# An image's six convolution pieces over four rounds: one, two, two, one

## The chip, the cores and the metric

The kernel runs on one core of a Trainium2 chip. The metric is the time on the device in microseconds, the median of three runs. All arithmetic is in 32-bit floats. Five engines work side by side, each with its own queue of instructions: TensorE (PE, with weight loads as PEld) for matrix products, VectorE (DVE), ScalarE (ACT) and GpSimd (POOL) for work on elements, and SyncE (SP), which here issues most of the DMA transfers. They wait for each other by semaphores.

## What is computed

The input is 16 images of 192 channels and 56 x 56 points. First comes a Swin block (windows of 7 x 7, shifted by 3, six heads), then a convolution whose weights depend on the image. Cut to what matters here:

```python
# layer 0: Swin block
h = roll(layernorm(x), (-3, -3))            # over channels
q, k, v = windows(h) @ qkv_w + qkv_b        # 64 windows of 49 tokens an image
a = softmax(q @ k.T * scale + bias + mask) @ v
x1 = x + roll(a @ proj_w + proj_b, (3, 3))
x2 = x1 + gelu(layernorm(x1) @ fc1_w + fc1_b) @ fc2_w + fc2_b

# layer 1: depthwise 3 x 3 convolution, weights made from the image
t = relu(batchnorm(mean(x2, over=(H, W)) @ w1.T))
wt = (t @ w2.T + b2).reshape(192, 3, 3) * MASK   # only 4 of 9 taps are not masked:
                                                 # three above, one to the left
out = depthwise_conv(x2, wt) + bias
```

The convolution of an image needs the mean over the whole image, and so it can start only when the Swin block of that image is finished.

## The kernel before

An image is handled in four steps of 14 rows (two rows of windows), 64 steps in all. The main loop is a software pipeline over rounds `i` from 2 to 65. In round `i` the MLP of step `i-2`, the attention of step `i`, the query, key and value products of step `i+1` and the norms of other steps are interleaved. The loop sets the order of the instructions on each engine by hand.

```python
for i in range(2, NS + 2):                     # NS = 64
    A, B_, C, D = pairs                        # four pairs of PSUM banks, in turn
    cs = conv_ready(2)                         # <- the line of the change
    ys = [conv_begin(*c) for c in cs[:1]]      # first piece: start, on ACT
    if has(i + 1):
        norm1_scale(i + 1, dvs.pop(0), nc.vector)   # win <- x,dv on DVE

    def after():
        ys.extend(conv_begin(*c) for c in cs[1:])   # second piece: start, on ACT
        for c, y in zip(cs, ys):
            conv_rest(*c, y)                        # three taps each, on DVE

    if (i + 3) % STEPS == 0 and (i + 3) // STEPS < B:    # STEPS = 4
        b = (i + 3) // STEPS
        images[b] = load_x(b, nc.sync)         # three images are held at a time

    def between():
        singles[0] = banks(f"st_{i}", C)
        keys.update(stats_of(i))               # PE: st <- x,sel and st <- sq,sel
        if keys:
            var.append(norm_vars(keys))        # ACT: square into dev; DVE: dev <- st,dev
    ...
    mlp_first(i - 2, yns.pop(i - 2), hid, (A, B_, C, D, A, B_), after, between)
    ...
    if has(i):
        top, share = attention_scores(i, *qs.pop(i), (C, D, A, B_))   # PE: sc <- kbd,q
    ...   # products q, k, e; softmax; second half of the MLP (pf); projection (pp); pv
    if (i - 2) % STEPS == STEPS - 1:           # an image's last step: its weights
        pt = taps(b, ...)                      # four matmuls on PE
        convs.append({"b": b, "n": 0})
    ...
    if has(i):
        residual(i, pp, pair1, at)             # DVE
    if has(i + 1):
        v_whole()
        attention_v_out(pvs)                   # vbd <- pv on DVE and ACT
    if has(i):
        norm_squares(f"2_{i}", i, 1, nc.scalar)
    if pt is not None:
        taps_rows(b)                           # DVE copies of border rows
        convs[-1]["wt"] = taps_out(b, convs[-1]["tt"])   # DVE: tw, wt
c = convs.pop()                                # the last image, after the loop
for n in range(6):
    conv_rest(c["b"], c["wt"], n, conv_begin(c["b"], c["wt"], n))
```

The first matrix product of the MLP frames both `after` and `between`:

```python
def mlp_first(i, yn, hid, ks, after, between):
    ...
    for f in range(3):
        take(f)
        long(dsts[f], wf1, cols(f), y0, True)      # PE: ph <- yn,wf
    for f in range(3):
        short(dsts[f], wf1, cols(f), y1, False)
        gelu(f)                                    # ACT: hid <- ph
    after()                                        # the convolution's pieces
    for f in range(3, NFC):
        take(f)                                    # banks that a Gelu has to free
        short(dsts[f], wf1, cols(f), y1, True)
    between()                                      # st, dev
    for f in range(3, NFC):
        long(dsts[f], wf1, cols(f), y0, False)
        gelu(f)
```

An image's convolution is cut into six pieces of 14 rows: four on the tall tile `x0` (channels 0 to 127, all 56 rows) and two on the half-height tile `x1` (the other 64 channels, its two halves side by side on 128 partitions). A piece takes one instruction on ACT (the first tap with the bias) and three on DVE; pieces three and five (counted from zero) have a small copy besides. The result goes out by DMA.

```python
def conv_ready(k):
    ready = []
    while k and convs and "wt" in convs[0]:
        c = convs[0]
        ready.append((c["b"], c["wt"], c["n"]))
        c["n"] += 1
        k -= 1
        if c["n"] == 6:
            convs.pop(0)
    return ready

def conv_begin(b, wt, n):
    kc, lo = (0, n * PR) if n < 4 else (1, (n - 4) * PR)     # PR = 14
    y = work.tile([128, PR, IMG], F32, tag="y", name=f"y_{b}_{n}", bufs=3)
    nc.scalar.activation(y, images[b][kc][:, lo : lo + PR], AF.Identity,
                         bias=cb[kc], scale=wt[:, kc, 1:2])
    return y

def conv_rest(b, wt, n, y):
    ...
    def tap(t, dst, src):
        nc.vector.scalar_tensor_tensor(
            dst, src, wt[:, kc, t : t + 1], dst, ALU.mult, ALU.add)
    tap(0, y[:, :, 1:], up[:, :, : IMG - 1])
    tap(2, y[:, :, : IMG - 1], up[:, :, 1:])
    ...
    tap(3, y[:, :, 1:], cur[:, :, : IMG - 1])
    ...                                                       # DMA to out
```

The weights of image `b` are made at the end of round 4b+5. Its pieces run in rounds 4b+6, 4b+7 and 4b+8, two in each; round 4b+9 has none. In that round the load of image b+3 is issued, into the buffers that image `b` held.

Of the kernel before, what the change touches and what calls it, by code (L numbers as in the profile page):

```python
# [36 lines left out]
def tile_swin_then_dynamic_conv(  # L37
# [45 lines left out]
    def banks(name, k):  # L83
        return psum.tile([128, 2, 512], F32, tag=f"pair{k}", name=name)
# [14 lines left out]
    def load_x(b, queue):  # L99
        t0, t1 = new_x(b)  # L100
        queue.dma_start(t0[:, 1 : 1 + LAST], x[b, 0:C0, SHIFT:IMG])
        queue.dma_start(t0[:, 1 + LAST : 1 + IMG], x[b, 0:C0, 0:SHIFT])
        queue.dma_start(t1[0:64, 1 : 1 + HALF], x[b, C0:DIM, SHIFT : SHIFT + HALF])
        queue.dma_start(t1[64:128, 1 : 1 + LAST - HALF], x[b, C0:DIM, SHIFT + HALF : IMG])
        queue.dma_start(t1[64:128, 1 + LAST - HALF : 1 + HALF], x[b, C0:DIM, 0:SHIFT])
        return t0, t1
# [206 lines left out]
    def norm1_scale(i, dv, engine):  # L313

        v0, v1 = rows_of(i)
        b4 = dv.rearrange("p h (r c) -> p h r c", c=IMG)
        w0 = win0[:, :, :, 0:N].rearrange("p h w (r c) -> p h r w c", c=WS)
        w1_ = win1[:, :, 0:N].rearrange("p w (r c) -> p r w c", c=WS)
        cut = WS - SHIFT
        for ws, cs, at, n in (  # L320
            (slice(0, NWIN - 1), slice(0, WS), SHIFT, NWIN - 1),
            (slice(NWIN - 1, NWIN), slice(0, cut), IMG - cut, 1),
            (slice(NWIN - 1, NWIN), slice(cut, WS), 0, 1),
        ):
            m = n * (cs.stop - cs.start)

            def wide(v):
                return v[..., at : at + m]

            for h in range(2):  # L330
                engine.tensor_tensor(
                    w0[:, h, :, ws, cs],
                    wide(v0[:, h]).rearrange("p r (w c) -> p r w c", w=n),
                    wide(b4[:, h]).rearrange("p r (w c) -> p r w c", w=n),
                    ALU.mult,
                )
            for h in range(2):
                p = slice(h * 64, h * 64 + 64)
                engine.tensor_tensor(  # L339
                    w1_[p, :, ws, cs],  # L340
                    wide(v1[p]).rearrange("p r (w c) -> p r w c", w=n),
                    wide(b4[p, h]).rearrange("p r (w c) -> p r w c", w=n),
                    ALU.mult,
                )
# [344 lines left out]
    def conv_begin(b, wt, n):  # L689

        kc, lo = (0, n * PR) if n < 4 else (1, (n - 4) * PR)
        y = work.tile([128, PR, IMG], F32, tag="y", name=f"y_{b}_{n}", bufs=3)
        nc.scalar.activation(  # L693
            y,
            images[b][kc][:, lo : lo + PR],
            AF.Identity,
            bias=cb[kc],
            scale=wt[:, kc, 1:2],
        )
        return y  # L700

    def conv_rest(b, wt, n, y):
        kc, lo = (0, n * PR) if n < 4 else (1, (n - 4) * PR)
        xk, cbk = images[b][kc], cb[kc]
        up, cur = xk[:, lo : lo + PR], xk[:, lo + 1 : lo + 1 + PR]

        def tap(t, dst, src):
            nc.vector.scalar_tensor_tensor(  # L708
                dst, src, wt[:, kc, t : t + 1], dst, ALU.mult, ALU.add
            )  # L710

        tap(0, y[:, :, 1:], up[:, :, : IMG - 1])
        tap(2, y[:, :, : IMG - 1], up[:, :, 1:])

        if n in (3, 5):
            p = slice(0, 128) if kc == 0 else slice(64, 128)
            nc.vector.tensor_copy(
                y[p, LAST - 3 * PR, :], cbk[p].broadcast_to([p.stop - p.start, IMG])
            )
        tap(3, y[:, :, 1:], cur[:, :, : IMG - 1])  # L720
        halves = [(slice(0, 128), slice(0, C0), lo)]
        if kc:
            halves = [(slice(h * 64, h * 64 + 64), slice(C0, DIM), lo + h * HALF) for h in range(2)]
        for p, c, at in halves:
            k = min(PR, LAST - at)
            nc.sync.dma_start(out[b, c, at + SHIFT : at + SHIFT + k], y[p, 0:k])
            if k < PR:
                nc.sync.dma_start(out[b, c, 0 : PR - k], y[p, k:PR])
# [8 lines left out]
    yns, convs, qs, dvs = {}, [], {}, {}  # L737

    def has(i):
        return 0 <= i < NS  # L740
# [12 lines that stand above are left out]
# [234 lines left out]
    for i in range(2, NS + 2):  # L987
        A, B_, C, D = pairs
        keys = {}


        cs = conv_ready(2)
        ys = [conv_begin(*c) for c in cs[:1]]
        if has(i + 1):
            norm1_scale(i + 1, dvs.pop(0), nc.vector)

        def after():
            ys.extend(conv_begin(*c) for c in cs[1:])
            for c, y in zip(cs, ys):
                conv_rest(*c, y)  # L1000

        if (i + 3) % STEPS == 0 and (i + 3) // STEPS < B:
            b = (i + 3) // STEPS
            images[b] = load_x(b, nc.sync)

        def between():
            singles[0] = banks(f"st_{i}", C)
            keys.update(stats_of(i))
            if keys:
                var.append(norm_vars(keys))  # L1010

        var = []
        hid = one.tile([128, NFC, 2, T], F32, tag="hid", name=f"hid_{i - 2}")
        mlp_first(i - 2, yns.pop(i - 2), hid, (A, B_, C, D, A, B_), after, between)
        for part, dev in var:
            table(AF.Sqrt)
            norm_root(part)


        outs = [lambda: None] * 4  # L1020
        if has(i):
            table(AF.Exp)
            top, share = attention_scores(i, *qs.pop(i), (C, D, A, B_))
        if has(i + 1):
            qs[i + 1], outs = attention_qk(i + 1, C, D, A)
        if has(i):
            top(0)
        outs[0]()
        if has(i):
            top(1)  # L1030
            share(0)
        outs[1]()
        if has(i):
            top(2)
            share(1)
        outs[2]()
        if has(i):
            top(3)
            share(2)
        outs[3]()  # L1040
        if has(i):
            share(3)
        for part, dev in var:
            nc.vector.reciprocal(part, part)
            dvs.update(norm_spread(keys, dev))

        prts = []

        def turn(f):
            for wp in ((), (), (), (0,), (1,), (2, 3))[f]:
                if has(i):
                    prts.append(attention_turn(i, wp, (C, A)[wp % 2]))

        pf = mlp_wide(i - 2, hid, B_, turn)
        mlp_out(i - 2, 0, pf[:, :, :T])
        table(AF.Gelu)
        if 1 in keys:
            yns[i - 1] = norm2_scale(i - 1, dvs.pop(1))  # L1060
        if has(i + 3):
            norm_squares(f"1_{i + 3}", i + 3, 0, nc.gpsimd)
        if has(i):
            o = attention_rows(i, attention_values(i, prts, D, C))
        pf1 = mlp_narrow(i - 2, hid, A)
        mlp_out(i - 2, 1, pf1[:, :T])
        if has(i):
            pp, pair1, p_narrow, p_rest, p_whole = project(i, o, B_, C)
            p_narrow()
            p_rest()  # L1070
        if has(i + 1):
            pvs, v_rest, v_whole = attention_v(i + 1, (D, A))
            v_rest()
        if has(i):
            p_whole()
        b, pt, at = (i - 2) // STEPS, None, lambda: None
        if (i - 2) % STEPS == STEPS - 1:
            pt = taps(b, taps_pool(b), pair1[:, 1] if has(i) else banks(f"t_{b}", C)[:, 0])
            convs.append({"b": b, "n": 0})

            def at():
                convs[-1]["tt"] = taps_hidden(b, pt)

        if has(i):
            residual(i, pp, pair1, at)
        else:
            at()
        if has(i + 1):
            v_whole()
            attention_v_out(pvs)  # L1090
# [3 lines that stand above are left out]
            taps_rows(b)  # L1094
            convs[-1]["wt"] = taps_out(b, convs[-1]["tt"])
        pairs = [C, B_, D, A]
# [77 lines left out]
```

## Time and profile before

| | |
|---|---|
| time, median of 3 runs | 3253.55 us (3251.41 to 3253.6) |
| span of the profiled run | 3251.8 us |
| clock granted to PE, mean | 0.986 |
| a tap of the convolution on DVE (L708) | 288 of them, 314.0 us busy, 1104 ns mean |
| DVE `dev<-st,dev`, 64x392 (L285) | two a round, 0.57 us each |
| HBM traffic | 41.25 MB read, 38.54 MB written, 25 GB/s over the span |

In the profile a group of instructions is named by its line, its engine, and what it writes and reads with buffer numbers left out: `ph<-yn,wf` is the first product of the MLP, `st<-x,sel` the sums for the norms, `dev` the variance, `sc<-kbd,q` the attention's scores, `y<-x,wt,y` a tap of the convolution. Most matmuls have the same line, L92, since a helper issues them, so they are told apart by tile. In a timeline, neighbouring instructions of one kind are put together: the first column is the start in us from the beginning of the span, the second the time to the end of the last of them, and xN their number. In square brackets stands how long the engine was idle before it, and who ended that wait.

### The profile page before, as it was taken

The numbers are of one execution on the slowest core, as the hardware profiler recorded it, in microseconds if no ns is written. First come the engines' busy times: TensorE is split into PE (matmuls) and PEld (weight loads), VectorE is DVE, ScalarE is ACT, GpSimd is POOL, SyncE is SP. The second block draws the span as 40 slices with busy tenths as digits, with TensorE's granted clock in tenths as the row PEclk, the third lists the DMA queues.
The fourth block names the chain that finished last, engine by engine and source line by source line (L and its number), as shares of the span: only waits on it lengthen the run. The fifth ranks groups of instructions, "written<-read, shape, count | busy, mean of one in ns | idle before, by whom it ended". The sixth has DMA issues, their size and how long they took to land.

```text
span 3251.8 us, 64181 instructions
## 1 busy us (share of the span) xinstructions
PE 3123.3 (96%) x26130; PEld 1937.1 (60%) x26130; DVE 2115.2 (65%) x3895; ACT 1887.8 (58%) x2988; POOL 991.6 (30%) x897
## 2 busy tenths in 40 slices
PE   5699999999999999999999999999999999999996
PEld 3556666666656656666666656666665665666653
DVE  5355675766766575685676666576676667667564
ACT  2455665655655665565565565565565666566552
POOL 5333233233223323323323323323323322322220
PEclk9699999999999999999999999999999999999998
DMA  3001011111111202112111201112111121211001
GB/s 99 16 15 51 25 37 51 37 55 31 40 52 32 60 31 61 31 31 56 36 52 40 58 26 40 51 35 56 31 37 55 31 59 32 61 30 32 22 30 45
DMA packets 79123, 135.35 MB, mean 42 GB/s; under 512 B 21766, under 2 KB 61692, under 8 KB 76908
## 3 DMA queue, kind: packets, MB, share of 16 engines
q1 hardware_dynamic: 77266, 128.54, 14.0%
q8 instruction: 206, 3.38, 0.4%
q0 software_dynamic: 1056, 1.92, 0.3%
q10 hardware_dynamic: 506, 0.79, 0.1%
q14 instruction: 89, 0.73, 0.1%
HBM read 41.25 MB, written 38.54 MB: 25 GB/s over the span
## 4 chain that ended last, share of the span: by engine, by line
PE 85%; DVE 9%; issue 2%; POOL 1%; ACT 0%; DMA 0%; SPq 0%; DVEq 0%; POOLq 0%; ACTq 0%
PE pf L92 23%; PE ph L92 19%; PE pp L92 7%; PE pv L92 6%; PE po L92 6%; PE pt L508 4%; PE pq L92 4%; PE sc L92 4%; PE pk L92 4%; PE pe L92 4%; PE st L92 3%; DVE y L708 3%; DVE win L339 1%; DVE vbd L451 1%; DVE x L584 1%
## 5 line engine op out<-in xcount | busy, mean ns | idle before, releaser
L92 PE MATMUL ph<-yn,wf 128*128 128x392 f32 (+1 forms) x3072 | 808.8, 501 | 9.3 <-ACT hid L598 3.5
L92 PE MATMUL pf<-hid,wf 128*128 128x392 f32 (+1 forms) x3072 | 802.8, 494 | 3.5 <-ACT hid L598 2.0
L495 POOL TENSOR_TENSOR prob<-e,tot 113x588 f32<-113x588 f32 x256 | 298.6, 1177 | 1205.6 <-DVE tot L494 1190.0
L92 PEld LDWEIGHTS ph<-yn,wf 128*128 128x128 f32 (+1 forms) x3072 | 424.7, 188 | 365.0 <-issue 83.9
L451 ACT COPY vbd<-pv 49x192 f32<-49x192 f32 x512 | 160.6, 314 | 704.2 <-DVE vbd L451 699.5
L92 PEld LDWEIGHTS pf<-hid,wf 128*128 128x128 f32 (+1 forms) x3072 | 386.3, 164 | 303.7 <-issue 120.0
L644 DVE SCALAR_TENSOR_TENSOR x<-pf,cols,x 128x784 f32<-128x784 f32 (+1 forms) x128 | 106.1, 829 | 537.8 <-PE pf L92 508.7
L598 ACT ACTIVATE hid<-ph,f1b 128x784 f32<-128x784 f32 x384 | 337.2, 913 | 115.1 <-PE ph L92 114.0
L253 POOL TENSOR_TENSOR sq<-sq,sq 64x392 f32<-64x392 f32 x256 | 263.7, 1030 | 369.5 <-ACT sq L247 354.9
L708 DVE SCALAR_TENSOR_TENSOR y<-x,wt,y 128x770 f32<-128x770 f32 x288 | 314.0, 1104 | 16.6 <-ACT y L693 8.4
L350 POOL TENSOR_TENSOR yn<-x,dv 128x784 f32<-128x784 f32 x64 | 119.0, 1859 | 571.3 <-DMA dv<-dev 549.1
L92 PEld LDWEIGHTS pv<-wqkv,win 64*128 64x128 f32 (+1 forms) x2048 | 258.1, 190 | 35.1 <-ACT kbd L405 2.8
L92 PE MATMUL pv<-wqkv,win 64*128 64x192 f32 (+1 forms) x2048 | 274.8, 327 | 3.3 <-ACT kbd L405 2.5
L486 DVE TENSOR_TENSOR e<-e,top 113x588 f32<-113x588 f32 x256 | 267.1, 1043 | 8.9
L92 PE MATMUL pp<-o,wp 128*128 128x392 f32 (+2 forms) x896 | 251.5, 514 | 2.7 <-ACT o L544 2.7
L489 ACT ACTIVATE e<-e 113x588 f32<-113x588 f32 x256 | 176.7, 691 | 132.9 <-DVE e L486 132.9
L238 ACT ACT_TABLE_LOAD x192 | 246.3, 1283 | 3.4
L514 ACT COPY prt<-pt 128x678 f32<-128x678 f32 x256 | 179.3, 727 | 117.2 <-PE pt L508 115.7
L479 DVE TENSOR_TENSOR e<-sc,bias_t 113x588 f32<-113x588 f32 x256 | 179.9, 763 | 100.5 <-PE sc L92 100.3
L508 PEld LDWEIGHTS pt<-ident,prob 113*128 113x128 f32 x1536 | 167.3, 142 | 77.8 <-issue 48.7
L92 PE MATMUL po<-prt,vbd 128*64 128x49 f32 x6144 | 199.9, 225 | 0.0
L92 PEld LDWEIGHTS po<-prt,vbd 128*64 128x64 f32 x6144 | 191.9, 140 | 9.4 <-ACT prt L514 0.6
(146 smaller groups left out, 3987.0 us busy)
## 6 DMA issues: line engine op xcount, KB each, us to landing
dv<-dev SPq DMA_DIRECT2D x1020, 49.0 KB
x<-in_x_dram SPq DMA_DIRECT2D x15, 1484.0 KB
out_dram<-y SPq DMA_DIRECT2D x48, 392.0 KB
out_dram<-y SPq DMA_DIRECT2D x48, 196.0 KB
x<-in_x_dram SPq DMA_DIRECT2D x16, 392.0 KB
x<-in_x_dram SPq DMA_DIRECT2D x15, 350.0 KB
out_dram<-y SPq DMA_DIRECT2D x16, 308.0 KB
out_dram<-y SPq DMA_DIRECT2D x16, 154.0 KB
```

The costliest lines, as they stand in the source:

```text
L92: nc.tensor.matmul(dst, lhs, rhs, start=start, stop=stop, skip_group_check=True)
L238: nc.scalar.activation(junk, eps_t[0:1], func)
L253: nc.gpsimd.tensor_tensor(s0[p, h], s0[p, h], s1[p], ALU.add)
L451: copy(dst, src[s * 64 : s * 64 + N, h, :, :, j, :])
L479: nc.vector.tensor_tensor(e, sc[:PW, :, : HEADS * N], rel, ALU.add)
L486: nc.vector.tensor_tensor(ehs[wp], ehs[wp], t.broadcast_to([PW, 2 * HEADS, N]), ALU.subtract)
L489: nc.scalar.activation(es[wp], es[wp], AF.Exp)
L495: nc.gpsimd.tensor_tensor(prob[wp][:PW, :, 0:N], ehs[wp], t.broadcast_to([PW, 2 * HEADS, N]), ALU.mult)
L508: nc.tensor.transpose(pt[:, a, g * PW : (g + 1) * PW], prob[wp][:PW, h : h + 2, :].rearrange("p h k -> p (h k)"), ident[:PW, :PW],)
L514: nc.scalar.copy(prt, pt[:, :, : 3 * PW])
L598: nc.scalar.activation(hid[:, f], phs[f][:, :, :T], AF.Gelu, bias=f1b[:, f : f + 1])
L708: nc.vector.scalar_tensor_tensor(dst, src, wt[:, kc, t : t + 1], dst, ALU.mult, ALU.add)
```

## The change

In the round in which an image's first piece is due, one piece is taken in place of two. The other rounds still take up to two, so that the six pieces fall on four rounds as one, two, two and one, and the last of them lies in round 4b+9, which had none. It is meant to take work off VectorE in the round that follows the making of the weights. Nothing is added or left out; every instruction stays as it was, and some move to a later round.

```diff
-        cs = conv_ready(2)
+        cs = conv_ready(1 if convs and not convs[0]["n"] else 2)
```

The pieces after the loop, of the last image, are not touched.

## The prediction

> **What bounds the kernel now.** I read the page first, then the list of waits, then the trace cut into rounds, and last the timelines of two rounds side by side.
>
> ```profile
> PE 3123.3 (96%) x26130; PEld 1937.1 (60%) x26130; DVE 2115.2 (65%) x3895; ACT 1887.8 (58%) x2988; POOL 991.6 (30%) x897
> PE 85%; DVE 9%; issue 2%; POOL 1%; ACT 0%; DMA 0%; SPq 0%; DVEq 0%; POOLq 0%; ACTq 0%
> ```
>
> TensorE (PE) is busy for 96% and carries 85% of the chain that ended last. VectorE (DVE) is busy for 65% only and yet holds 9% of the chain: there are places where it decides. The waits view names one that bears on this change:
>
> ```profile
> PE sc L92 <- DVE dev L285: 23.1, 15, 1.5
> ```
>
> The scores' matmuls waited 23.1 us in total for the DVE instruction `dev`, 15 times, 1.5 us each. Fifteen is the number of images whose convolution runs inside the loop (0 to 14), so it happens once an image. To see where, I cut the trace at each start of a group of score matmuls. A stretch then runs from the attention of one round to the first matrix product (`ph`, `st`, `ph`) of the next, in which the pieces run. Columns: stretch, its length, and busy time and count of PE, PEld, DVE, ACT and POOL, then clock, DMA share and GB/s.
>
> ```profile
> 1592.67:1640.34 47.67, 47.67 (x407) 29.66 (x406) 34.04 (x60) 29.78 (x47) 14.85 (x13) 1.00 0.12 32
> 1640.34:1688.02 47.68, 47.68 (x408) 29.69 (x407) 27.00 (x53) 27.92 (x45) 14.84 (x13) 1.00 0.26 75
> 1688.02:1738.40 50.38, 48.61 (x411) 29.93 (x411) 35.89 (x67) 31.27 (x49) 15.07 (x13) 1.00 0.10 29
> 1738.40:1786.08 47.68, 47.68 (x407) 29.67 (x407) 34.05 (x60) 28.28 (x46) 14.85 (x13) 1.00 0.12 36
> ```
>
> These stretches hold the pieces of rounds 32 (two pieces, the image's last), 33 (none), 34 (the next image's first two) and 35 (two more). Two pieces or none, a stretch takes 47.68 us and PE is full: pieces are free there. Only the stretch with an image's first two takes longer, by 2.70 us. There are fourteen more like it: thirteen are within 0.02 us of it, and the last takes 49.72 us against 47.01 us for the stretch after it, 2.71 more. Now PE in the long stretch, and below it DVE and ACT there (start, duration, what, idle before):
>
> ```profile
> 1728.86 1.74 PE L92 MATMUL ph<-yn,wf 64*128 64x392 f32 x8 [0.23 <-ACT hid L598]
> 1730.53 1.52 PE L92 MATMUL st<-x,sel 128*32 128x392 f32 x16
> 1731.87 0.84 PE L92 MATMUL st<-sq,sel 128*32 128x392 f32 x8
> 1732.64 4.22 PE L92 MATMUL ph<-yn,wf 128*128 128x392 f32 x12
> 1738.40 2.24 PE L92 MATMUL sc<-kbd,q 64*64 64x98 f32 x96 [1.54 <-DVE dev L285]
> ```
> ```profile
> 1724.91 0.56 DVE L674 SCALAR_TENSOR_TENSOR tw<-tt,w2n 128x384 f32<-128x384 f32 x1
> 1725.51 0.55 DVE L683 TENSOR_REDUCE wt<-tw 128x8 f32<-128x384 f32 x1
> ...
> 1730.90 6.18 DVE L708 SCALAR_TENSOR_TENSOR y<-x,wt,y 128x770 f32<-128x770 f32 x6
> 1737.11 1.14 DVE L285 TENSOR_TENSOR dev<-st,dev 64x392 f32<-64x392 f32 x2
> ```
> ```profile
> 1732.87 0.99 ACT L283 ACTIVATE dev<-st 64x392 f32<-64x392 f32 x2 [1.51 <-PE st L92]
> ```
>
> `dev` has its inputs when ACT's square is done, at 1732.87 + 0.99 = 1733.86. It starts at 1737.11, because six taps (two pieces of three) stand before it in DVE's queue, and they begin late, at 1730.90, behind the new image's weights (`tw`, `wt`), which only this round computes. In round 32 the same queue is ahead of PE:
>
> ```profile
> 1631.61 5.93 DVE L708 SCALAR_TENSOR_TENSOR y<-x,wt,y 128x770 f32<-128x770 f32 x5
> 1637.58 0.19 DVE L717 COPY y<-cols 64x56 f32<-64x56 f32 x1
> 1637.80 1.02 DVE L708 SCALAR_TENSOR_TENSOR y<-x,wt,y 128x770 f32<-128x770 f32 x1
> 1638.85 1.14 DVE L285 TENSOR_TENSOR dev<-st,dev 64x392 f32<-64x392 f32 x2
> ```
>
> It ends at 1639.99, and the scores start at 1640.34 with no wait.
>
> [...] round 32's last `ph` group is given an end of 1640.42, and the next matmul starts at 1640.34. So I reckon with starts. [...] round 32's first tap starts at 1631.61 while POOL adds squares (1630.52 to 1632.62) and takes 1.84 us; the others take 1.02.
>
> **The change part by part.** Piece counts per image go from 2, 2, 2, 0 to 1, 2, 2, 1. Instructions are the same in number and shape; what moves is one piece out of each first round, one each between the others, and the last into a round that had none.
>
> 1. First round (34 and its like). DVE loses three taps of 1.02 us with gaps of about 0.03: 6.18 / 6 x 3 = 3.09 us. The last tap then ends at 1734.0. ACT's square ends at 1733.86, so `dev` runs from about 1734.05 to 1735.2. What would the scores then wait for? In an undisturbed stretch they follow the last `ph` group's start by 1640.34 - 1636.20 = 4.14 us. Here that group starts at 1732.64, so they may start at 1736.79 instead of 1738.40. `dev` is ready 1.5 us before. The gain is 1738.40 - 1736.79 = 1.61 us: half of the 3.09 us of taps was already beside PE's work.
>
> 2. The rest of the 2.70 us stays, 1.09 us. The taps' weights need four matmuls on PE, 0.4 us. The matmuls of `ph` wait for ACT's Gelu to free banks; ACT does the first piece's start (1.02 us) before the Gelu and comes late from its copies, since DVE is late: `st` starts 8.85 us after the first `ph` (1721.69, shown in the PE timeline as 1730.53) instead of 8.20 us, so 0.65 us. The first piece stays in this round and ahead of the Gelu, so this stays. New length of the stretch: 50.38 - 1.61 = 48.77 us.
>
> 3. Second and third rounds hold two pieces as before: 47.68 us each.
>
> 4. Last round (33, 37 and so on): one piece more on a DVE with 27.0 us busy of 47.7. Round 32 shows that two pieces in this place cost nothing, so one doesn't. ACT's start of a piece (about 1.03 us) also comes before the Gelu, as in round 32, where it costs nothing. Cost 0.
>
> 5. The third image after takes over this image's buffer, and its load is issued in that last round. The order of instructions shows a new wait: the load of the half-height tile `x1` now waits for DVE and ACT, for piece five still reads it; the load of the tall tile has no such wait. Before, the five loads are issued from 1667.78 to 1671.50. After, `x1` can go when the taps of round 33 are done, about 1679.3 + 3 x 1.05 + 0.8 (the first beside POOL) + 0.2 = 1683.5. Its first reader is POOL's square at 1717.86, 34 us later. About 0.8 MB at the 265 GB/s that the trace shows while an image comes in is 3 us. The queue behind it holds nothing urgent: the next copies of `dv` are issued at 1704.89. Cost 0.
>
> 6. The end. Image 14's last piece goes into round 65, in which ACT waits 17.9 us and DVE 25.0 us; image 15's six pieces after the loop are untouched. The taps there may meet POOL's scaling of `yn` (1.83 and 2.09 us from 3193.88), on which PE waits: up to 1 us, once. I count 0.
>
> Sum: 15 first rounds x 1.61 = 24.2 us. 3253.55 - 24.2 = 3229.4 us, 0.7% less.
>
> **The rivals.** First, the whole 2.70 us goes, 40 us in all and 3213 us. That would need the second piece to be what makes the Gelu late; against it, that piece's start on ACT comes after the three Gelus (1730.30 against 1727.90). Second, a first round still bound by DVE: if taps took 1.84 us each, as the one beside POOL, `dev` would end 2.5 us later and nearly all gain would go: 3250 us. Against it, POOL's last addition there ends at 1729.34, before the taps start. Third, the load becomes the wait: a late `x1` holds POOL's squares, then `st`. It has some 30 us in hand; if it did cost 1 us an image, the time would be 3245. Fourth, the piece in the round without pieces costs what it frees: 15 x 1.6 back, no change; rounds 32 and 35 speak against it.
>
> **Range and chances.** All steps are read from stretches that repeat to 0.02 us, and three runs lie within 2.2 us, so the doubt is in steps 2, 4 and 5. A loss of 0.4 us an image gives 6 us more, 3235; a gain of 0.3 us in step 2 gives 4.5 us less, 3225. I take 3225 to 3236. Two per cent are 65 us; PE's work alone forbids that gain. Faster by over 2%: 0.01; within: 0.98; slower: 0.01.
>
> **What would show it.** Right: `sc <- dev` gone from the waits; stretches of 48.8, 47.7, 47.7 and 47.7 us; three taps before `dev` in the first; `x1` loads some 12 us later than the tall tile's with POOL's squares where they were. Wrong: a first stretch of 47.7 (step 2), or of over 49 (step 1), a fourth over 48 (step 4), or a wait of POOL for `in_x_dram` (step 5).

## The result, and the profile after

The changed kernel takes 3229.15 us (median of 4 runs, 3228.76 to 3229.39), the kernel before in the same comparison 3253.57 us. The ratio is 0.9925, 95% interval 0.9908 to 0.9943: 24.4 us or 0.75% less. The prediction was 3229.4 us.

The page of the changed kernel, busy time by engine and the chain that ended last:

```profile
PE 3121.5 (97%) x26130; PEld 1936.5 (60%) x26130; DVE 2130.7 (66%) x3895; ACT 1886.0 (58%) x2988; POOL 992.1 (31%) x897
PE 89%; DVE 3%; ACT 2%; issue 1%; POOL 1%; DMA 0%; SPq 0%; ACTq 0%; DVEq 0%; POOLq 0%
```

The counts of instructions are the same. DVE's share of the chain fell from 9% to 3% while its busy time rose, by 15.5 us: a first hint that it was never DVE's total that mattered. The list of waits no longer has the row in which `sc` waits for `dev`, which stood there with 23.1 us. The stretches of rounds 32 to 35, in the columns used before:

```profile
1581.62:1629.30 47.68, 47.68 (x407) 29.66 (x406) 34.05 (x60) 29.75 (x47) 14.81 (x13) 1.00 0.11 30
1629.30:1676.98 47.68, 47.68 (x408) 29.67 (x407) 31.07 (x57) 28.82 (x46) 14.87 (x13) 1.00 0.26 74
1676.98:1725.75 48.77, 48.54 (x412) 29.91 (x411) 32.92 (x64) 28.82 (x46) 15.05 (x13) 1.00 0.13 35
1725.75:1773.42 47.67, 47.67 (x407) 29.66 (x406) 33.85 (x59) 29.75 (x47) 14.82 (x13) 1.00 0.11 33
```

The second line is the round that had no piece; DVE works 4.1 us more in it, and it is as long as before. The third is the first round of an image: 48.77 us instead of 50.38. PE, DVE and ACT in that stretch:

```profile
1717.82 1.73 PE L92 MATMUL ph<-yn,wf 64*128 64x392 f32 x8 [0.23 <-ACT hid L598]
1719.49 1.52 PE L92 MATMUL st<-x,sel 128*32 128x392 f32 x16
...
1721.60 4.22 PE L92 MATMUL ph<-yn,wf 128*128 128x392 f32 x12
1725.75 2.24 PE L92 MATMUL sc<-kbd,q 64*64 64x98 f32 x96
```
```profile
1719.87 3.13 DVE L708 SCALAR_TENSOR_TENSOR y<-x,wt,y 128x770 f32<-128x770 f32 x3
1723.03 1.14 DVE L285 TENSOR_TENSOR dev<-st,dev 64x392 f32<-64x392 f32 x2
```

Three taps stand before `dev` instead of six. It ends at 1724.17, and the scores follow the last `ph` group after 4.15 us, as in any other round, with no wait in brackets. The 0.23 us before the upper `ph`, from the late Gelu, are still there.

The sum over the loop: 14 first stretches of 1.61 us less and the last with 1.62 us less make 24.16 us. The rest of the 24.5 us between the two profiled spans is 0.40 us at the start, 0.51 us in the last stretch, and 0.45 us the other way: one stretch took 0.57 us more than its like, where before another took 0.12 more. Start and last stretch differ by a few microseconds between profiled runs (the start from 186.7 to 191.8 us, the last stretch from 110.1 to 115.1), so a hit to within 0.3 us in the total is partly luck. The stretches themselves are not. The last stretch goes with how often the granted clock fell to 0.5 for 3.41 us in it, before the last matmul: 110.1 to 111.0 us where it never did, 112.4 to 113.2 where it did once, as before and after the change, and 115.0 or 115.1 where it was low for longer.

### The profile page after: what moved, and what is told of

Same layout as the page of the kernel before. It is cut to its first block, busy times and chain, and to the rows that moved or that the text cites. A ratio compares the mean times of both kernels' runs of the same rounds, so it can differ in the third digit from the quotient of the medians.

```text
span 3227.3 us, 64171 instructions
## 1 busy us (share of the span) xinstructions
PE 3121.5 (97%) x26130; PEld 1936.5 (60%) x26130; DVE 2130.7 (66%) x3895; ACT 1886.0 (58%) x2988; POOL 992.1 (31%) x897
## 4 chain that ended last, share of the span: by engine, by line
PE 89%; DVE 3%; ACT 2%; issue 1%; POOL 1%; DMA 0%; SPq 0%; ACTq 0%; DVEq 0%; POOLq 0%
PE pf L92 23%; PE ph L92 21%; PE pp L92 7%; PE pv L92 6%; PE po L92 6%; PE pt L508 4%; PE pq L92 4%; PE sc L92 4%; PE st L92 4%; PE pe L92 4%; PE pk L92 4%; DVE vbd L451 1%; DVE x L584 1%; ACT hid L598 0%; ACT y L693 0%
## 5 line engine op out<-in xcount | busy, mean ns | idle before, releaser
L708 DVE SCALAR_TENSOR_TENSOR y<-x,wt,y 128x770 f32<-128x770 f32 x288 | 328.7, 1151 | 16.8 <-ACT y L693 8.2
L578 DVE SCALAR_TENSOR_TENSOR x<-pp,cols,x 128x371 f32<-128x371 f32 (+1 forms) x128 | 48.0, 417 | 227.8 <-PE pp L92 227.8
```

The source lines that it names most:

```text
L708: nc.vector.scalar_tensor_tensor(dst, src, wt[:, kc, t : t + 1], dst, ALU.mult, ALU.add)
```

## The experiments

All were timed beside the kernel before. "First stretch" is the one that ends in an image's first round, 50.38 us before and 48.77 us after; the second to fourth follow it.

| pieces, and what else is changed | time, us | first to fourth stretch, us |
|---|---|---|
| 2, 2, 2, 0 (before) | 3253.57 | 50.38, 47.68, 47.68, 47.67 |
| 1, 2, 2, 1 (the change) | 3229.15 | 48.77, 47.68, 47.68, 47.68 |
| 2, 2, 1, 1 | 3253.03 | 50.39, 47.68, 47.68, 47.68 |
| 2, 2, 2, 0, `dev` between the first two pieces | 3230.12 | 48.77, 47.74, 47.68, 47.68 |
| 1, 2, 2, 1, first start behind the Gelus | 3219.18 | 48.12, 47.68, 47.68, 47.68 |
| 0, 2, 2, 2 | 3219.06 | 48.12, 47.68, 47.68, 47.68 |
| 2, 2, 2, 0, first starts behind the Gelus | 3270.81 | 50.39, 49.29 (nine of fifteen), 47.68, 47.68 |
| 1, 3, 2, 0 | 3276.44 | 48.77, 50.52, 47.68 (four: 49.1 to 49.3), 47.68 |
| 1, 3, 2, 0, three taps done again | 3344.53 | 48.77, 53.68, 49.94, 47.68 |
| 1, 2, 2, 1, start behind the Gelus, weights twice | 3222.24 | 48.57, 47.68, 47.68, 47.67 |
| 1, 2, 2, 1, tall tile last | 3226.99 | 48.77, 47.68, 47.68, 47.68 |

The stretches are medians over the images.

**Only the first round had no room.** Two, two, one, one:

```diff
-        cs = conv_ready(2)
+        cs = conv_ready({2: 2, 3: 2, 0: 1, 1: 1}[i % STEPS])
```

> Two, two, one, one: six pieces over four rounds, as many rounds with one piece as in the change, but the first round keeps two. Theory (only the first round had no room): first stretch 50.4 us, the others 47.7 us, time 3253.5 us as before. Rival (it is the spreading over four rounds that pays, wherever the single pieces lie): about 3229 us.

3253.03 us, ratio 0.9997 (0.9988 to 1.0005). The first two stretches:

```profile
1685.68:1736.07 50.39, 48.61 (x411) 29.94 (x411) 35.89 (x67) 31.25 (x49) 15.04 (x13) 1.00 0.13 38
1736.07:1783.75 47.68, 47.68 (x406) 29.67 (x406) 34.03 (x60) 28.25 (x46) 14.83 (x13) 1.00 0.12 36
```

Nothing is gained by a piece in the fourth round as such. What pays is the piece missing from the first. The rival, spreading for its own sake, falls.

**The order in DVE's queue, or its load?** Two, two, two, none, but in the first round the second piece's taps stand after `dev`:

```diff
+        ahead = 1 if cs and cs[0][2] == 0 else 2
 ...
-            for c, y in zip(cs, ys):
+            for c, y in list(zip(cs, ys))[:ahead]:
                 conv_rest(*c, y)
 ...
                 var.append(norm_vars(keys))
+            for c, y in list(zip(cs, ys))[ahead:]:
+                conv_rest(*c, y)
```

> Two, two, two, none as before, but in an image's first round the three taps of the second piece stand after `dev` in DVE's queue. DVE does as much in that round as in the kernel before. Theory (what cost 1.61 us was `dev` standing behind the taps): `dev` starts near 1734.05 on the clock of the trace before and the scores are no longer held by it; the second piece's taps then end some 0.6 us later than DVE would have begun on the scores, which costs up to 0.3 us at the products that reuse those banks: first stretch 48.8 to 49.1 us, time 3229 to 3235 us. Rival (DVE had too much work in that round, in whatever order): the wait only moves to the scores' banks, the stretch and what follows it keep 2.7 us too many, 3253 us.

3230.12 us, ratio 0.9925 (0.9910 to 0.9940): the same gain as the change, though no piece left its round. DVE in the first stretch:

```profile
1719.59 3.13 DVE L708 SCALAR_TENSOR_TENSOR y<-x,wt,y 128x770 f32<-128x770 f32 x3
1722.75 1.14 DVE L285 TENSOR_TENSOR dev<-st,dev 64x392 f32<-64x392 f32 x2
1723.82 3.12 DVE L708 SCALAR_TENSOR_TENSOR y<-x,wt,y 128x770 f32<-128x770 f32 x3
1726.85 2.79 DVE L479 TENSOR_TENSOR e<-sc,bias_t 113x588 f32<-113x588 f32 x4
```

The same six taps, `dev` between them. The first stretch is 48.77 us. DVE begins on the scores 1.39 us after PE's start on them (1725.46), in the changed kernel 0.87 us, and this image's second stretch is 47.75 us instead of 47.68: the whole price of the late taps is 0.07 us. So the cost was `dev` in DVE's queue behind work that nobody waited for, and not too much work for DVE in that round.

**What is left in the first stretch: ACT.** The change, with the start of the first round's piece behind the three Gelus:

```diff
+        early = 0 if cs and cs[0][2] == 0 else 1
-        ys = [conv_begin(*c) for c in cs[:1]]
+        ys = [conv_begin(*c) for c in cs[:early]]
 ...
-            ys.extend(conv_begin(*c) for c in cs[1:])
+            ys.extend(conv_begin(*c) for c in cs[early:])
```

> One, two, two, one, and in an image's first round the start of the piece on ACT stands after the three Gelus instead of ahead of them. Theory (step 2: of the 1.09 us left in the first stretch, 0.65 us come from that start, 1.02 us on ACT, which makes the Gelu free banks late): the first `ph` to `st` takes 8.2 us instead of 8.85, the first stretch 48.1 us instead of 48.77, and the time is 3229.2 - 15 x 0.65 = 3219 us. Rival (the Gelu is late since ACT's copies are late behind DVE, whatever stands between): the stretch stays at 48.8 us and the time at 3229 us.

3219.18 us, ratio 0.9890 (0.9875 to 0.9905). And no piece at all in the first round, zero, two, two, two:

```diff
-        cs = conv_ready(2)
+        cs = conv_ready({2: 0, 3: 2, 0: 2, 1: 2}[i % STEPS])
```

> No piece in an image's first round, then two, two, two. Theory: the first stretch loses the piece's start on ACT ahead of the Gelu as well, so 48.1 us; two pieces in the fourth round are as free as in the second and third, 47.7 us; time 3219 us. If it comes out at 3229 us, ACT's lateness is not from the piece's start. Rival (the fourth round has less room, since the load of the half-height tile now waits for two pieces): fourth stretch over 48 us or POOL waiting for the input, and 3229 us or more.

3219.06 us, ratio 0.9889 (0.9872 to 0.9905). Its first and fourth stretch:

```profile
1672.16:1720.28 48.12, 48.12 (x411) 30.08 (x410) 29.85 (x61) 27.89 (x45) 15.05 (x13) 1.00 0.19 51
1815.64:1863.32 47.68, 47.68 (x407) 29.67 (x407) 34.03 (x60) 29.75 (x47) 14.83 (x13) 1.00 0.19 57
```

Both reach 48.12 us in the first stretch, 0.65 us less than the change; in both PE is busy for the whole of it. With the start behind the Gelus, `st` comes 8.19 us after the first `ph` instead of 8.84. So the 0.65 us were the start of a piece ahead of the Gelu. These two are better than the change by 10 us, and the fourth round takes two pieces for nothing.

**The same move without the change.** Two, two, two, none, with both starts behind the Gelus (the edit above, on the kernel before):

> Two, two, two, none as before, with both starts of an image's first round behind the three Gelus. Theory (two waits stand behind one another in the first stretch, and `dev` behind the taps ends last): `st` starts 0.65 us earlier and the scores wait that much longer for `dev`; first stretch 50.4 us, time 3253.5 us. Rival (the 0.65 us is worth its own gain): 49.7 us and 3244 us.

3270.81 us, ratio 1.0056 (1.0039 to 1.0073). The first stretch did what the theory said: `st` starts 41.86 us after the scores instead of 42.52, the scores wait 2.20 us for `dev` instead of 1.54, and the stretch is 50.39 us long. Two waits stand one behind the other; as long as `dev` ends last, the 0.65 us are worth nothing. But the total was 17 us over the forecast. Two of the fifteen gaps tell why: first PE's timeline at the end of each, then the stretches that follow them (the third number from the end is the granted clock):

```profile
1547.33 3.87 PE L92 MATMUL sc<-kbd,q 64*64 64x98 f32 x96 [2.20 <-DVE dev L285]
...
1742.37 2.24 PE L92 MATMUL sc<-kbd,q 64*64 64x98 f32 x96 [2.20 <-DVE dev L285]
```
```profile
1547.33:1596.63 49.30, 49.30 (x407) 31.30 (x407) 34.22 (x60) 27.47 (x46) 14.83 (x13) 0.97 0.12 36
1742.37:1790.05 47.68, 47.68 (x407) 29.67 (x407) 34.04 (x60) 27.61 (x46) 14.81 (x13) 1.00 0.12 36
```

The same 96 score matmuls take 3.87 us after one gap and 2.24 us after another. In the trace's clock records the clock is 0.5 for 3.41 us at 1547.31, and at eight more of the fifteen gaps. Each such stretch is 1.61 to 1.66 us longer, 14.7 us in all; the last stretch, 115.1 us in this run, holds 2.0 more than before. The start was 4.3 us shorter, so this run, at 3266.08 us, is 12.6 us over the forecast. The other three took 3269.57 to 3272.39 us at a mean clock of 0.975 to 0.978 against 0.982; the runs of the kernel before alone range from 0.981 to 0.988, and how often the clock fell in these three is not shown.

**How much room DVE has.** One, three, two, none:

```diff
-        cs = conv_ready(2)
+        cs = conv_ready({2: 1, 3: 3, 0: 2, 1: 0}[i % STEPS])
```

> One, three, two, none: the first round is light as in the change, the fourth has none as before, and the second takes the piece left over. Theory (DVE has room for two pieces before `dev` in a round, and no more: two leave `dev` ready 0.2 to 0.45 us before it is needed): three more taps of 1.02 us make the second stretch 47.7 + 3.1 - 0.3 = 50.5 us, with the scores waiting for `dev`; first stretch 48.8; time 3229.2 + 15 x 2.8 = 3271 us. Rival (what held the scores was the making of the weights in the round before, not the number of pieces): second stretch 47.7 us, 3229 us.

3276.44 us, ratio 1.0071 (1.0056 to 1.0086). Second and third stretch after one gap:

```profile
1937.66:1988.18 50.52, 47.75 (x408) 29.68 (x408) 37.02 (x63) 33.22 (x52) 14.83 (x13) 1.00 0.12 36
1988.17:2037.47 49.30, 49.30 (x406) 30.78 (x406) 34.29 (x60) 27.26 (x44) 14.90 (x13) 0.97 0.13 33
```

The second stretch is 2.84 us longer, as forecast: three taps of 3.1 us less the 0.3 us in hand, and the scores wait 2.77 us. With two pieces `dev` has 0.2 to 0.4 us to spare, so two are the limit of a round with no weights to make. The total is 5 us over the forecast. The clock fell again: to 0.5 after 5 of 15 gaps, which makes four of the third stretches 1.45 to 1.62 us longer, 6.2 us in all (the fifth fall lies in the last stretch).

**Is it the gap?** One, three, two, none, with the first tap of each of the three pieces done twice (`len(cs) // 3` is 1 in a round with three pieces and 0 in the others):

```diff
-        tap(0, y[:, :, 1:], up[:, :, : IMG - 1])
+        for _ in range(1 + again):
+            tap(0, y[:, :, 1:], up[:, :, : IMG - 1])
 ...
-                conv_rest(*c, y)
+                conv_rest(*c, y, len(cs) // 3)
```

> The run with one, three, two, none showed something that no theory had: after 5 of its 15 gaps of 2.77 us the granted clock of PE was 0.5 for 3.41 us, and the next stretch took some 1.5 us more. Here the first tap of each of the three pieces in the second round is done twice, so that the gap of PE there is some 3.1 us longer, 5.9 us (the output differs by the taps added again). Theory (a gap makes the clock drop [...]): the clock drops after all 15, each of the stretches that follow takes 1.5 to 1.7 us more, time 3229.2 + 15 x (2.84 + 3.1 + 1.6) = 3342 us. Rival (the drops have nothing to do with the gaps' length): about 5 of 15 again, 3327 us.

3344.53 us, ratio 1.0282 (1.0267 to 1.0298). The scores wait 5.93 us, and the clock falls after all 15 gaps. A second and a third stretch:

```profile
1782.29:1835.97 53.68, 47.75 (x408) 29.70 (x407) 40.08 (x66) 33.21 (x52) 14.83 (x13) 0.99 0.11 34
1835.97:1886.16 50.19, 50.19 (x407) 31.85 (x407) 34.44 (x60) 27.23 (x44) 14.83 (x13) 0.95 0.12 32
```

Third stretches take 1.4 to 2.9 us more than 47.68, 2.3 at the median, more than the 1.5 to 1.7 expected; the clock was low for 6.83 us, and not 3.41, in 13 of the 15 cases. With the clock low after all 15, the rival (5 of 15 again) falls.

**The matmuls of the weights.** As the run with the start behind the Gelus, with these matmuls done twice:

```diff
-        for kc in range(2):
+        for kc in (0, 1, 0, 1):
```

> As the run that moved the piece's start behind the Gelu, with the matmuls of the weights done twice (the second pass begins the sum anew). Theory (of the 0.44 us by which that run's first stretch is still longer than the others, 0.4 are these matmuls, on a PE that waits for nothing): first stretch 48.5 us, time 3219.2 + 15 x 0.4 = 3225 us. Rival (the 0.44 us are DVE's lateness, and the matmuls lie beside it): 48.1 us and 3219 us.

3222.24 us, ratio 0.9905 (0.9891 to 0.9920). The first stretch is 48.57 us, 0.45 more than 48.12, so these matmuls are the whole of the last 0.44 us. The total rose by 3 us and not by 6.7: between the two profiled runs the last stretch was 2.3 us shorter here (110.1 us against 112.4, where the clock fell once) and the start 0.9 us shorter.

**The load that waits.** The change, with the pieces in the order 4, 5, 0, 1, 2, 3, so that the tall tile is read last:

```diff
-            ready.append((c["b"], c["wt"], c["n"]))
+            ready.append((c["b"], c["wt"], (4, 5, 0, 1, 2, 3)[c["n"]]))
```

> One, two, two, one, with the pieces in another order: the two of the half-height tile first, the four of the tall tile after them, so that it is the large load (1.5 MB, and what follows it in the queue) that has to wait for the last piece. Theory (step 5: the load has some 30 us in hand): all loads of an image are issued some 15 us later than before the change, POOL's squares start where they did, 3229 us. Rival (the late load becomes the wait): POOL waits for the input and the fourth stretch grows, 3235 us or more.

3226.99 us, ratio 0.9919 (0.9903 to 0.9936), the change within the spread of start and end. The queue in the fourth round, first in the changed kernel, then in this run:

```profile
1657.00 0.58 SPq L101 DMA_DIRECT2D x<-in_x_dram  x1
1657.62 1.63 SPq L102 DMA_DIRECT2D x<-in_x_dram  x1
1672.47 0.52 SPq L103 DMA_DIRECT2D x<-in_x_dram  x1
```
```profile
1672.93 0.35 SPq L101 DMA_DIRECT2D x<-in_x_dram  x1
```

With the whole image held back by 15 us, the four stretches are 48.77, 47.68, 47.68 and 47.68 us, and POOL waits for no image but the very first, as in the kernel before.

## Why the prediction was right

1. The first round: three taps in 3.13 us with their gaps (3.09 predicted), `dev` 1.58 us ahead of need, 1.61 us gained in each of fifteen. Right, and the run with `dev` between the pieces shows that the cause is the queue's order.

2. The 1.09 us that stays: right in size and in its parts. Behind the Gelus the start costs nothing, and the 0.65 us are gone; doubled, the weights' matmuls cost 0.45 us. The prediction named two reasons for the late Gelu, the start and ACT's late copies. It takes both: without the start the late copies cost nothing (48.12 us with PE full), and in the other rounds, where ACT is less late, the same start costs nothing (round 32: the Gelus begin 5.51 us after the first `ph` instead of 6.21, and the stretch takes 47.67 us).

3. Second and third rounds: 47.68 us, unchanged.

4. The fourth round costs nothing with one piece, nor with two.

5. The load: no cost, and none even with the whole image held back. One number was careless. The note on what would show it said that the half-height tile's load would come "some 12 us" after the tall tile's; it came 15.5 us after. The working itself has 1667.78 and 1683.5, which makes 15.7; 12 us is the distance from 1671.50, where all five loads had been issued.

6. The end: POOL's two scalings of the half-height tile took 3.42 us instead of 2.09 beside the taps, but PE needed only the tall tile's at once; its wait there was 2.41 us, 2.26 before.

Of the rivals, that the whole 2.70 us would go failed on the 0.44 us of matmuls and on the piece's start ahead of the Gelu. DVE still binding, the late load, and the fourth round paying it all back are each excluded by the stretches. The working of the second was off: taps of 1.84 us would have put the end of `dev` 3 x 0.82 = 2.46 us later, at 1737.66, which is still 0.59 us before the 1738.25 of the kernel before. So some 9 us of the gain would have stayed, 3245 us and not 3250.

Nor does PE's work alone forbid a gain of 65 us, as the range had it: 3123.3 us of it leave 128 in the span. What forbids it is that a stretch without the wait is full of PE's work, so that the first rounds can give 15 x 2.70 = 40.5 us at most.

## What to carry to other kernels

Compare rounds that should be alike, start to start: the one that is longer shows what a wait costs, and the equal ones show which work is free where. In a queue that runs in order, as DVE's did here (`dev`, ready at 1733.86 us in the kernel before, started at 1737.11 behind six taps), ask of each instruction who waits for it, and put work that nobody waits for behind the one that the busiest engine needs; that gave as much here (3230.12 us) as moving the work to another round (3229.15 us). Before moving something off a second wait, make sure that the first no longer ends last: the same edit gained 10 us after the change, and before it gained nothing in its stretch, made the gap longer (2.20 us instead of 1.54), and cost 17 us, with the clock falling after nine of the fifteen gaps in the profiled run.

## What was not expected

Short gaps in PE's work cost more here than themselves, when the granted clock fell after them:

| run | gap, us | clock fell | clock at 0.5 for, us | next stretch longer by, us |
|---|---|---|---|---|
| 2, 2, 2, 0 (before) | 1.54 | 0 of 15 | | |
| 2, 2, 2, 0, first starts behind the Gelus | 2.20 | 9 of 15 | 3.41 | 1.61 to 1.66 |
| 1, 3, 2, 0 | 2.77 | 5 of 15 | 3.41 | 1.45 to 1.62 (four; the fifth fall lies in the last stretch) |
| 1, 3, 2, 0, three taps done again | 5.93 | 15 of 15 | 6.83 in 13 cases | 1.4 to 2.9 |

In the kernel before the clock stays at 1.00 from 178.7 us to 3196.0 us, over all its fifteen gaps. The gaps of 2.20 us met a fall more often than those of 2.77 us, and of two gaps of 2.20 us, shown above, one was followed by a fall and the other was not. So the length of a gap alone does not tell whether the clock falls after it; what else it goes with is not shown.
